# Transposing norms and probabilities by VectorE blocks and a DRAM detour instead of by TensorE, in a Perceiver block

## The chip, the cores and the metric

The kernel runs on one core of one Trainium2 chip. The metric is the device time of one execution in microseconds (us). A profile shows one execution: its span runs from the first to the last instruction, and the time of that execution is a little longer than the span. The engines are TensorE (PE, whose weight loads the profile lists apart as PEld), VectorE (DVE), ScalarE (ACT), GpSimd (POOL) and SyncE (SP, which here only issues DMAs).

## The reference

One layer over 16 batches, all in float32. Each batch has 128 tokens of 512 features and a context of 2048 rows of 512 features.

```
x = x + xattn(layernorm(x), ctx)     # softmax(h ctx^T) ctx: no scale, no projection
x = x + attn(layernorm(x), ...)      # 16 heads of 32; q, k, v by down and up weights;
                                     # rotary on half of each head; causal softmax; @ Wc
h = layernorm(x)
x = x + h + sum_e gate_e * (h A_e^T) Bw_e^T   # 8 experts of rank 64; the top 2 by the logits
                                              # of the batch's first token
```

In this setup the batch length S equals 128, so one batch of tokens fills the 128 partitions of one tile.

## The kernel before

The work is written as four Python generators per batch: `score` (first norm, context scores, softmax numerators), `attend` (product with the context, first residual, second norm), `inner` (self-attention, second residual, third norm) and `experts` (routing and the two chosen experts). A hand-written list of `step(kind, b)` calls at the end of `perceiver_block` interleaves the pieces of several batches. TensorE's instructions are kept in that written order (`tc.keep_in_program_order`), so TensorE runs them one after another in exactly that order, and a matmul whose input is late holds up all later ones. The DVE, ACT and POOL queues are ordered by the framework near the written order, and each engine works through its queue in order as well. In the steady part of the loop the loads on SP are not held to the written order (`written = False`).

For each batch TensorE does, by the names that the profile shows:

- `psc`: context scores, 4 tiles of 512 context rows, 16 matmuls each, from the transposed context `ctxT` (loaded) and the transposed norm `hT`;
- `tr_m` and `spread`: a shared maximum per token, turned and spread over the partitions; `den`: the softmax denominators;
- `av`: probabilities times context, 4 tiles `ctx`, 4 matmuls each;
- `q`, `k`, `v`: projections of the second norm with weights folded at the start (`fold_*`); `pss_sc`, `pss_acc`: the scores of 16 heads; `y`: probabilities times values per head; `o`: the output projection;
- `lg`: the 8 router logits; `mid`, `ffn`: the two experts;
- `tr` and `tr_p_a`: transposes by a matmul against the identity. Every float32 matmul is two passes in the profile, a transpose is one.

The transposes work in groups of four 128x128 blocks. `transposed(src, dst, name)` turns a norm of 128x512 into one PSUM bank and ScalarE copies the bank to SBUF (`hT1` for the first norm, `hT2` for the second, `hT3` for the third). `turn` does the same for four heads of the attention probabilities `att`, four times a batch. The attention softmax of a batch runs on DVE and ACT in four groups of four heads: mask add, maximum, 16 exponentials with sums on ACT, reciprocal, multiply.

The routing goes: `hT3` (its first column is the first token) -> `shares` on DVE (`g_share`, `g_part`) -> the matmul `lg` -> about a dozen small DVE instructions -> two indirect DMAs on POOL for the rows of `A` and one for `BT`. `early` does this routing for the last batch from the value row of the first token, ahead of the rest.

Buffers that matter: `ctx` and `ctxT` have four tiles of 1 MB each, so each tile can be loaded again as soon as the TensorE work on its predecessor is over; `ps_acc` has three PSUM banks and `ps_sc` two.

Of the kernel before, what the change touches and what calls it, by code (L numbers as in the profile page):

```python
# [29 lines left out]
SCALE = 1.0 / math.sqrt(DH)  # L30
NEG = -1e30


C_ID, C_MASK, C_COS, C_SIN, C_BLK = 0, 128, 256, 384, 512


C_ONE, C_TWO, C_ONER, C_TWOR, C_RANK, C_P = 514, 515, 516, 517, 518, 519
C_N = 520
# [4 lines left out]
def constants():  # L43

    c = np.zeros((P, C_N), np.float32)
    c[:, C_ID : C_ID + P] = np.eye(P)
# [20 lines left out]
def perceiver_block(ctx: ExitStack, tc: tile.TileContext, io: dict, out: bass.AP):  # L67
# [6 lines left out]
    p4 = ctx.enter_context(tc.tile_pool(name="p4", bufs=4))  # L74
    ps_tr = ctx.enter_context(tc.tile_pool(name="ps_tr", bufs=3, space=PSUM))
# [5 lines left out]
    ident = cst[:, C_ID : C_ID + P]  # L81
# [13 lines left out]
    written = True  # L95

    def load(*args):
        dma = nc.sync.dma_start(*args)
        if written:
            tc.keep_in_program_order(dma)  # L100
# [7 lines left out]
    def layernorm(src, name, n=P, tag="h"):  # L108
        stats = p2.tile([P, 6], F32, tag="stats", name=f"st_{name}")[:n]
        nc.vector.bn_stats(stats, src)  # L110
        mv = p2.tile([P, 2], F32, tag="mv", name=f"mv_{name}")[:n]
        nc.vector.bn_aggr(mv, stats)  # L112
        rstd = p2.tile([P, 1], F32, tag="rstd", name=f"rs_{name}")[:n]
        nc.gpsimd.tensor_scalar_add(rstd, mv[:, 1:2], EPS)  # L114
        nc.gpsimd.tensor_tensor(rstd, rstd, mhalf[:n], ALU.pow)  # L115
        h = (p2 if tag == "h" else p1).tile([P, D], F32, tag=tag, name=f"{tag}_{name}")[:n]
        nc.vector.tensor_scalar(h, src, mv[:, 0:1], rstd, ALU.subtract, ALU.mult)  # L117
        return h

    def transposed(src, dst, name, at=(0, 1, 2, 3)):  # L120

        tr = bank(ps_tr, "tr", f"tr_{name}")
        for c, i in enumerate(at):
            transpose(tr[:, c * P : (c + 1) * P], src[:, i * P : (i + 1) * P], ident)
        nc.scalar.copy(dst, tr.rearrange("p (c t) -> p c t", c=4))  # L125

    def turn(src, at, name):
        t = p4.tile([P, 4, P], F32, tag="pT", name=f"pT_{name}")
        transposed(src, t, f"p_{name}", at)
        return t  # L130
# [21 lines left out]
    def fold_products(i, n, g):  # L152
# [8 lines left out]
        folded = []  # L161
        for j, ps in enumerate(banks):
            t = p4.tile([P, D], F32, tag="pT", name=f"folded_{n}_{g}_{j}")
            (nc.vector.tensor_copy if j else nc.scalar.copy)(t, ps)
            folded.append(t)
        return folded
# [39 lines left out]
    def score(b):  # L206
# [3 lines left out]
        hT = p2.tile([P, KC, S], F32, tag="hT1", name=f"hT1_{b}")  # L210
        transposed(h, hT, f"1_{b}")
# [4 lines left out]
        for v, ct in enumerate(turned_cts.pop(b)):  # L216
            ps = bank(ps_sc, "sc", f"psc_{b}_{v}").rearrange("p (j t) -> p j t", j=4)
            for j in range(4):
                for c in range(KC):
                    matmul(  # L220
                        ps[:, j, :], ct[:, c, j * P : (j + 1) * P], hT[:, c, :],
# [62 lines left out]
    def inner(b):  # L284

        x1, h = firsts.pop(b)
        hT = p1.tile([P, KC, S], F32, tag="hT2", name=f"hT2_{b}")
        transposed(h, hT, f"2_{b}")
        yield

        heads_first = {}
        for n in ("q", "k"):
            ps = bank(ps_acc, "acc", f"{n}_{b}")
            for m in range(HC):
                for c in range(KC):
                    matmul(
                        ps[:, m * P : (m + 1) * P], w[n][:, c, m * P : (m + 1) * P], hT[:, c, :],
                        start=(c == 0), stop=(c == KC - 1),
                    )
            partner = p1.tile([P, HC, S], F32, tag=f"{n}P", name=f"{n}P_{b}")  # L300
            nc.vector.stream_shuffle(partner.rearrange("p c t -> p (c t)"), ps, PARTNERS)
            t = p1.tile([P, HC, S], F32, tag=f"{n}T", name=f"{n}T_{b}")
# [8 lines left out]
            heads_first[n] = t  # L311
            yield
        qT, kT = heads_first["q"], heads_first["k"]
        vv = p2.tile([P, D], F32, tag="vv", name=f"vv_{b}")
        att = p1.tile([P, H, S], F32, tag="att", name=f"att_{b}")
        nmx = p2.tile([P, H], F32, tag="nmx", name=f"nmx_{b}")
        sm = p2.tile([P, H], F32, tag="sm", name=f"sm_{b}")
        rsm = p2.tile([P, H], F32, tag="rsm", name=f"rsm_{b}")

        def project():  # L320

            ps = bank(ps_acc, "acc", f"v_{b}")
            for c in range(KC):
                matmul(ps, hT[:, c, :], w["v"][:, c, :], start=(c == 0), stop=(c == KC - 1))
            nc.scalar.copy(vv, ps)
            values[b] = (x1, vv)

        def compare():
# [25 lines left out]
            for group, ps in enumerate(pss):  # L354
# [17 lines left out]
                )  # L372


        for part in (project, compare) if b < B - 1 else (compare, project):
            part()
            yield

        flat = att.rearrange("p h t -> p (h t)")

        def heads(c):
            first = c // 2 * 8 + c % 2 * 2
            return first, first + 1, first + 4, first + 5

        now = [turn(flat, heads(c), f"a_{b}_{c}") for c in range(HC)]
        yield
        acc = bank(ps_acc, "acc", f"y_{b}")
        for c in range(HC):
            for j in range(4):
                at = c * P + j * DH  # L390
                matmul(
                    acc[j * DH : (j + 1) * DH, c * P : (c + 1) * P],
                    vv[:, at : at + DH], now[c][:, j, :], start=True, stop=True,
# [70 lines left out]
    def early(b):  # L464


        x1, vv = values[b]
# [8 lines left out]
        column = column_of(vv[:1, :], f"v0_{b}")  # L476
        v0 = small(b, KC, "v0")
        nc.vector.tensor_copy(v0, column)
# [13 lines left out]
    def experts(b):  # L492

        x2, h = lasts.pop(b)
        res = p2.tile([P, D], F32, tag="res", name=f"res_{b}")
        nc.gpsimd.tensor_tensor(res, x2, h, ALU.add)
        hT = p2.tile([P, KC, S], F32, tag="hT3", name=f"hT3_{b}")
        transposed(h, hT, f"3_{b}")
        yield
        if b not in routes:  # L500
            route(b, shares(b, hT[:, :, 0]))
# [3 lines left out]
        for c in range(KC):  # L505
            matmul(ps[:, :S], wa[:, c, :], hT[:, c, :], start=(c == 0), stop=(c == KC - 1))
# [3 lines left out]
        o = p2.tile([P, D], F32, tag="o", name=f"out_{b}")  # L510
# [24 lines left out]

    load_x(0)
    load_turned(0, [0])
    load_x(1)
    load_turned(0, [1, 2, 3])
    for v in range(VC):  # L540
        load_turned(1, [v])
        load_ctx(0, [v])
    load(up, io["up"])
    step(score, 0, 5)
    step(score, 1, 2)
    step(score, 0)
# [8 lines left out]
    step(score, 1)  # L555
    step(attend, 0)
    step(score, 1)
    load_weight("v", "ctx")
    step(attend, 0, 2)
    load_x(2)  # L560
    step(score, 2)
# [10 lines left out]
    for i, n, g in halves:  # L572
# [3 lines left out]
        ready = (n, g, folded)  # L576
    step(inner, 0)
    fold_turned(*ready)

    written = False  # L580
    for b in range(B - 2):
        if 2 < b + 2 < B:
            load_turned(b + 2)
        step(inner, b, 2)
        step(experts, b - 1)
        step(score, b + 2)
        step(inner, b)
        step(experts, b - 1)
        step(score, b + 1)
        step(score, b + 2, 2)  # L590
        step(attend, b + 1)
        step(inner, b)
        step(score, b + 2)
        step(attend, b + 1)
        step(score, b + 2)
        step(attend, b + 1)
        step(inner, b)
        step(score, b + 2)
        step(attend, b + 1)
        if b + 2 < B:  # L600
            load_ctx(b + 2)
        if b + 3 < B:
            load_x(b + 3)
        step(inner, b)
        step(experts, b - 1)
        step(inner, b)
        step(inner, b + 1)
        step(experts, b - 1)
        step(score, b + 3)
# [3 lines left out]
    step(inner, y)  # L613
    step(score, z)
    step(inner, y)
    step(experts, y - 1)
    step(inner, y)
    step(experts, y - 1)
    step(attend, z)
# [7 lines left out]
    step(inner, z, 2)  # L627
    step(inner, y)
    step(inner, z, 2)
    step(experts, y)  # L630
    step(early, z)
    step(experts, y)
    step(early, z)
    step(inner, z)
    step(early, z)
    step(inner, z)
# [46 lines left out]
```

## Time and profile before

| what | value |
|---|---|
| time, median of 3 runs (lowest, highest) | 880.22 us (880.09, 880.26) |
| time of the profiled execution | 879.31 us |
| its span | 875.8 us |
| PE busy | 846.8 us, 97% of the span |
| PEld, DVE busy | 615.6 us, 511.5 us |
| ACT, POOL busy | 270.9 us, 171.3 us |
| granted TensorE clock, mean over the span | 0.991 of full speed |
| DMA | 159.57 MB, mean 182 GB/s |
| HBM read, written | 154.47 MB, 4.19 MB |

The profile's page gives, part by part: busy time of each engine, the span in 40 slices, the DMA queues, the chain of work that ended last, groups of equal instructions with their mean duration and the wait ahead of them, and the DMA issues with the time to landing. The trace can also be asked for a timeline of one engine, for the sums of a window, and for the waits of one engine for another.

### The profile page before, as it was taken

Reading aid. Unit: us, or ns where it says so; the run is one execution under the profiler, and the core shown is the slowest. Engines: PE = TensorE matmul, PEld = TensorE weight load, DVE = VectorE, ACT = ScalarE, POOL = GpSimd, SP = SyncE. Lnnn points to the kernel's source line nnn. Section 1 sums busy time; section 2 is a strip of 40 time slices with the busy share of each in tenths; the row PEclk is TensorE's granted clock in tenths of the full one; section 3 lists DMA queues with packets and bytes.
Section 4 is the critical chain, followed back from the end, with each engine's and each line's share of the span. In section 5 each row is a group of like instructions: output and inputs, shape, how many; then the busy total and the mean of one; then the engine's idle time right before and its main releaser. Section 6 shows DMA issues by size and latency. Waiting matters only on the chain.

```text
span 875.8 us, 14131 instructions
## 1 busy us (share of the span) xinstructions
PE 846.8 (97%) x5498; PEld 615.6 (70%) x5498; DVE 511.5 (58%) x1234; ACT 270.9 (31%) x829; POOL 171.3 (20%) x232
## 2 busy tenths in 40 slices
PE   5999999999999999999999999999999999998966
PEld 4958767677777768677776867777686777765733
DVE  1436557375755747575574757557475755738472
ACT  1213314224232422423242242324224232422341
POOL 1001021130313103031310403121040312103123
PEclk9999999999999999999999999999999999999987
DMA  6997735637183563618356361835637183241001
GB/s 270 414 377 303 277 116 205 223 133 243 69 296 133 200 222 138 241 71 296 133 197 225 132 245 71 294 136 195 227 133 245 68 295 126 74 144 36 13 24 49
DMA packets 29553, 159.57 MB, mean 182 GB/s; under 512 B 4144, under 2 KB 4400, under 8 KB 13104
## 3 DMA queue, kind: packets, MB, share of 16 engines
q1 hardware_dynamic: 25392, 146.09, 45.7%
q0 software_dynamic: 4096, 12.59, 3.9%
q8 instruction: 43, 0.70, 0.3%
q14 instruction: 22, 0.18, 0.1%
HBM read 154.47 MB, written 4.19 MB: 181 GB/s over the span
## 4 chain that ended last, share of the span: by engine, by line
PE 93%; DVE 3%; POOL 1%; ACT 1%; issue 1%; DMA 1%; SPq 0%; ACTq 0%; POOLq 0%
PE psc L89 27%; PE av L89 25%; PE o L89 7%; PE q L89 6%; PE k L89 6%; PE v L89 5%; PE tr_p_a L92 3%; PE tr L92 2%; PE y L89 2%; PE pss_sc L89 2%; PE mid L89 2%; PE pss_acc L89 1%; PE ffn L89 1%; ACT att L365 1%; DMA x<-in_x_dram 1%
## 5 line engine op out<-in xcount | busy, mean ns | idle before, releaser
L89 PEld LDWEIGHTS psc<-hT,ctxT 128*128 128x128 f32 x2048 | 235.9, 193 | 12.9 <-DVE att L356 4.6
L89 PE MATMUL psc<-hT,ctxT 128*128 128x128 f32 x2048 | 240.2, 277 | 0.7 <-ACT hT L125 0.7
L89 PE MATMUL av<-ctx,sc 128*128 128x512 f32 x512 | 230.4, 593 | 0.0
L89 PEld LDWEIGHTS av<-ctx,sc 128*128 128x128 f32 x512 | 93.1, 192 | 92.9 <-issue 92.9
L365 ACT ACTIVATE att<-att,nmx 128x128 f32<-128x128 f32 x256 | 99.0, 389 | 113.8 <-DVE nmx L363 113.8
L114 POOL TENSOR_SCALAR rs<-mv 128x1 f32<-128x1 f32 x48 | 10.3, 226 | 435.4 <-DVE mv L112 435.0
L125 ACT COPY hT<-tr 128x512 f32<-128x512 f32 x48 | 26.8, 586 | 174.3 <-PE tr L92 174.3
L224 ACT COPY sc<-psc 128x512 f32<-128x512 f32 x64 | 37.1, 580 | 102.4 <-PE psc L89 101.9
L89 PEld LDWEIGHTS q<-hT,w_q 128*128 128x128 f32 x512 | 58.4, 192 | 10.2 <-ACT hT L125 10.2
L89 PE MATMUL q<-hT,w_q 128*128 128x128 f32 x512 | 61.3, 278 | 0.7 <-ACT hT L125 0.7
L89 PE MATMUL o<-w_c,yT 128*128 128x512 f32 x128 | 60.2, 615 | 0.9 <-ACT yT L396 0.9
L117 DVE TENSOR_SCALAR h<-x,mv,rs 128x512 f32<-128x512 f32 x48 | 39.3, 818 | 36.8 <-POOL rs L115 35.8
L89 PE MATMUL k<-hT,w_k 128*128 128x128 f32 x512 | 59.8, 275 | 0.0
L89 PEld LDWEIGHTS k<-hT,w_k 128*128 128x128 f32 x512 | 58.5, 192 | 0.0
L89 PE MATMUL v<-w_v,hT 128*128 128x512 f32 x128 | 57.7, 593 | 0.0
L441 POOL DMA_INDIRECT each<-in_A_dram,g_blocks x32 | 35.5, 1109 | 99.2 <-DVE g_dn L458 94.4
L125 ACT COPY pT_a<-tr_p_a 128x512 f32<-128x512 f32 x64 | 32.9, 600 | 53.0 <-PE tr_p_a L92 52.9
L365 ACT ACTIVATION_READ_ACCUMULATOR att<-att,nmx 128x1 f32 x256 | 48.2, 188 | 0.0
L356 DVE TENSOR_TENSOR att<-pss_sc,cst 128x512 f32<-128x512 f32 x32 | 20.6, 684 | 46.8 <-PE pss_sc L89 46.8
L249 DVE TENSOR_TENSOR sc<-sc,spread 128x512 f32<-128x512 f32 x64 | 42.6, 678 | 5.2 <-PE spread L89 5.2
L252 ACT ACTIVATE sc<-sc 128x512 f32<-128x512 f32 x64 | 40.2, 631 | 16.6 <-DVE sc L249 15.7
L370 DVE TENSOR_TENSOR att<-att,rsm 128x512 f32<-128x512 f32 x64 | 44.1, 689 | 1.1
(125 smaller groups left out, 952.3 us busy)
## 6 DMA issues: line engine op xcount, KB each, us to landing
ctxT<-in_ctxT_dram SPq DMA_DIRECT2D x64, 1024.0 KB, 4.8
ctx<-in_ctx_dram SPq DMA_DIRECT2D x64, 1024.0 KB, 4.8
x<-in_x_dram SPq DMA_DIRECT2D x16, 256.0 KB, 4.8
out_dram<-out POOLq DMA_DIRECT2D x15, 256.0 KB, 2.4
down_q<-in_Wq_downT_dram SPq DMA_DIRECT2D x2, 1024.0 KB, 11.4
down_k<-in_Wk_downT_dram SPq DMA_DIRECT2D x2, 1024.0 KB, 7.8
down_v<-in_Wv_downT_dram SPq DMA_DIRECT2D x2, 1024.0 KB, 7.9
w_c<-in_Wc_dram SPq DMA_DIRECT2D x1, 1024.0 KB, 13.3
```

What stands on the lines that cost most here:

```text
L89: tc.keep_in_program_order(nc.tensor.matmul(*args, **kwargs))
L92: tc.keep_in_program_order(nc.tensor.transpose(*args))
L114: nc.gpsimd.tensor_scalar_add(rstd, mv[:, 1:2], EPS)
L117: nc.vector.tensor_scalar(h, src, mv[:, 0:1], rstd, ALU.subtract, ALU.mult)
L125: nc.scalar.copy(dst, tr.rearrange("p (c t) -> p c t", c=4))
L224: nc.scalar.copy(sc[:, v], ps)
L249: nc.vector.tensor_tensor(sc[:, v], sc[:, v], spread[:, None, :S].to_broadcast([P, 4, S]), ALU.add)
L252: nc.scalar.activation(sc[:, v], sc[:, v], AF.Exp)
L356: nc.vector.tensor_tensor(att[:, hs, :], ps.rearrange("p (h t) -> p h t", h=4), cst[:, None, C_MASK : C_MASK + S].to_broadcast([P, 4, S]), ...
L365: nc.scalar.activation(att[:, i, :], att[:, i, :], AF.Exp, bias=nmx[:, i : i + 1], scale=SCALE, accum_out=sm[:, i : i + 1],)
L370: nc.vector.tensor_tensor(att[:, hs, :], att[:, hs, :], rsm[:, hs, None].to_broadcast([P, 4, S]), ALU.mult)
L441: nc.gpsimd.indirect_dma_start(each[:, i, :], None, io["A"], bass.IndirectOffsetOnAxis(ap=blocks[:, i : i + 1], axis=0),)
```

## The change

Four things change together.

**Who transposes.** For most batches `transposed` no longer uses TensorE and ScalarE. VectorE transposes the 32x32 blocks inside each group of 32 partitions (`nc.vector.transpose`, one instruction for 128x512), into a tile `blocks` (for norms) or `pX` (for probabilities, two groups of four heads each). `send` then writes the four groups of partitions to a DRAM tile `there` with four DMAs, and `fetch` reads it back with one DMA, so that each block reaches the partitions where it belongs. All five go onto SP's queue. This is done for `hT1` of batches 1 to 15, `hT2` of batches 0 to 14, `hT3` of batches 0 to 13, and the probabilities of batches 0 to 13 (two halves a batch). The remaining transposes, at the start and in the last two batches, stay on TensorE.

**Layouts.** The turned tiles are now laid out by group of 32 tokens (`hT[p, a, c, j]`). The matmuls that stream them read them with a stride. `v`, which loads them as weights, is split into four column groups: 16 matmuls of 32 weight columns in place of 4 of 128.

**The order.** The step list is new: `v` ahead of `k` and `q`; all four `psc` tiles of a batch in a row; `y` of batch b after the `psc` tiles of batch b+2; the router's `lg` of batch b-1 between the second `av` tile of batch b+1 and the head scores of batch b; and the loads, sends and fetches on SP all held to the written order. For the first two norms POOL's steps are held to the order in which they are written.

**Small edits.** The identity is a tile of its own, loaded by ScalarE's queue; `early` computes the first token's values with 16 matmuls of one column from `hT2`; several tiles have one buffer where they had two.

```diff
+    def send(name):
+        if name not in ways:
+            return
+        blocks, dst = ways[name]
+        n = blocks.shape[2]
+        there = dram.tile([4, QD, 4, n * QD], F32, tag=f"there_{n}", name=f"there_{name}")
+        for a in range(4):
+            load(
+                there[:, :, a, :].rearrange("q i e -> i q e"),
+                blocks[a * QD : (a + 1) * QD].rearrange("i q n j -> i q (n j)"),
+            )
+        ways[name] = there, dst
+
+    def fetch(name):
+        if name in ways:
+            there, dst = ways.pop(name)
+            load(dst.rearrange("p a n j -> p (a n j)"), there.rearrange("q i a e -> (q i) (a e)"))
...
+        else:
+            blocks = p1.tile([P, 4, n, QD], F32, tag="blocks", name=f"blocks_{name}")
+            nc.vector.transpose(blocks, src.rearrange("p (n q i) -> p q n i", n=n, q=4))
+            ways[name] = blocks, dst
...
+            ps = bank(ps_acc, "acc", f"v_{b}")
+            for c in range(KC):
+                for a in range(4):
+                    matmul(
+                        ps[a * QD : (a + 1) * QD, :], hT[:, a, c, :], w["v"][:, c, :],
+                        start=(c == 0), stop=(c == KC - 1),
+                    )
...
+                if group % 2 == 0:
+                    blocks = p2.tile([P, 4, H // 2, QD], F32, tag="pX", name=f"pX_{b}_{group}")
+                nc.vector.transpose(
+                    blocks[:, :, group % 2 * 4 : group % 2 * 4 + 4, :],
+                    att[:, hs, :].rearrange("p n (q i) -> p q n i", q=4),
+                )
+                if group % 2:
+                    ways[f"p_{b}_{group // 2}"] = blocks, pT[group // 2]
...
     for b in range(B - 2):
...
         step(inner, b, 2)
         step(experts, b - 1)
+        send(f"3_{b - 1}")
+        if b:
+            load_turned(b + 2, [0])
+        fetch(f"3_{b - 1}")
+        if b:
+            load_turned(b + 2, [1, 2, 3])
+        step(attend, b + 1, 2)
+        load_ctx(b + 2, [0, 1])
+        step(experts, b - 1)
+        step(inner, b)
+        step(attend, b + 1)
+        load_ctx(b + 2, [2])
+        step(attend, b + 1)
+        step(inner, b + 1)
+        send(f"p_{b}_0")
+        load_ctx(b + 2, [3])
+        fetch(f"p_{b}_0")
+        send(f"2_{b + 1}")
+        send(f"p_{b}_1")
+        fetch(f"2_{b + 1}")
+        fetch(f"p_{b}_1")
+        if b + 3 < B:
+            load_x(b + 3)
+        step(score, b + 2, 4)
+        step(inner, b)
+        step(inner, b + 1)
         step(score, b + 2)
         step(experts, b - 1)
+        step(score, b + 3, 2)
+        send(f"1_{b + 3}")
+        fetch(f"1_{b + 3}")
         step(inner, b)
         step(score, b + 2)
         step(experts, b - 1)
```

The steps of `inner` in the changed kernel are, in this order: turning the second norm, `v`, `k`, `q`, the head scores with their softmax, (in the last two batches turning the probabilities,) `y`, `o`. Those of `experts` are: turning the third norm, routing, `mid`, `ffn`.

## The prediction

> **What bounds the kernel now.** I read the busy times and the chain of waits first, then one steady batch as a window, then that batch on the PE timeline, then the tail's waits beside the granted clock, last the DMA issues. A change of 0.2% (1.8 us) is about what a measurement of this kernel can tell from none.
>
> ```profile
> PE 846.8 (97%) x5498; PEld 615.6 (70%) x5498; DVE 511.5 (58%) x1234; ACT 270.9 (31%) x829; POOL 171.3 (20%) x232
> PE 93%; DVE 3%; POOL 1%; ACT 1%; issue 1%; DMA 1%; SPq 0%; ACTq 0%; POOLq 0%
> ```
>
> ```profile
> 338.20:389.35 51.15, 51.15 (x336) 37.60 (x335) 31.61 (x76) 16.46 (x52) 10.62 (x14) 1.00 0.52 186
> ```
>
> The window is one batch, from one `psc` start to the next: PE is busy all 51.15 us, DVE 31.6, DMA 52%. So the steady part is bound by PE, and a batch costs what PE does in it. PE work that goes is gained whole; a PE wait that appears is lost whole, because TensorE keeps the written order.
>
> **What is removed.** The PE timeline of that batch:
>
> ```profile
> 364.92 1.97 PE L92 MATMUL tr_p_a<-cst,att 128*128 128x128 f32 x16
> 366.72 0.32 PE L92 MATMUL tr_m<-cst,mx 128*128 128x128 f32 x1
> ...
> 370.41 1.08 PE L89 MATMUL y<-pT_a,vv 128*32 128x128 f32 x32
> ...
> 375.85 0.60 PE L92 MATMUL tr<-cst,h 128*128 128x128 f32 x4
> 376.29 1.02 PE L89 MATMUL ffn<-wb,mid 128*128 128x512 f32 x2
> 377.18 3.84 PE L89 MATMUL q<-hT,w_q 128*128 128x128 f32 x32
> 380.86 3.74 PE L89 MATMUL k<-hT,w_k 128*128 128x128 f32 x32
> ```
>
> From start to next start, the 16 transposes of probabilities take 1.80 us and four of a norm 0.44. A batch loses 1.80 + 3 x 0.44 = 3.1 us of PE, so 51.15 becomes 48.05. The seven ACT copies that go (0.59 each) cost nothing, ACT being idle 68% of the batch.
>
> **What costs nothing, or little.** `v` becomes 32 passes of 32 weight columns by 512. If the four column groups overlap, it stays at 3.44 us; if not, 4 x 3.44. `y` has that shape of weights: 32 passes in 1.08 us, 0.27 of it the last one's latency, so 25 ns each, where `q` needs 3.68 / 32 = 115 ns for as many columns. They overlap, so 3.44; the other end, +10.3 us a batch, is a rival. The extra DMA is 7 transfers of 256 or 512 KB a batch each way, 3.5 MB on 9.5 (186 GB/s x 51.15): 13.0 MB in 48 us is 271 GB/s, and this trace moved 427 for 10 us, so bandwidth holds. The seven DVE transposes appear nowhere in the trace. The nearest row, the shuffle of 128x512, has 0.72 us, net 0.62 between starts; half or twice that moves DVE by 2 to 5 us of some 36 in 48. I take 0.62, and count them only on the two paths below.
>
> **The wait added at `lg`.** The listing of the built program shows the queues. On DVE, after `o` of batch b: residual, third norm, the softmax adds and sums of batch b+2, `k` rotation, `q` shuffle and multiply, and only then the transpose of the third norm. On SP: four sends, the load of `ctxT` tile 0, the fetch of `hT3`. Then DVE `g_share`, `g_part`, and PE `lg`; behind `lg` wait the head scores, the rest of `av` and all later PE work. Before, `hT3` came from PE directly and `v` covered its routing.
>
> PE gets from the end of `o` to `lg` in spread 0.3 + ffn 0.9 + k and q 7.3 + two `av` 6.9 = 15.4 us. The other way:
> - DVE: 17 full-width operations at 0.61 net (two mask adds start 349.90 and end 1.29 later), 0.8 for small ones, 0.2 to start: 11.4.
> - Sends: an SP issue takes 0.33 to 0.43; the fourth starts 1.2 later and lands 1.8 after that (the small output store): 14.4.
> - Fetch: 256 KB alone lands in 2.7. Here 1 MB went ahead at 12.9 and lands 4.8 later, at 17.7; the rest is behind it, 0.65 at 400 GB/s: 18.4. Alone, 17.1.
> - `g_share` 0.93 and `g_part` 0.18: 19.5.
>
> So `lg` comes 4.1 us late; with a freer queue and faster DVE 2.5, with DVE at its recorded 0.69 each 5.5.
>
> ```profile
> x<-in_x_dram SPq DMA_DIRECT2D x16, 256.0 KB, 4.8
> ...
> out_dram<-out SPq DMA_DIRECT2D x2, 128.0 KB, 1.8
> ```
>
> ```profile
> ctxT<-in_ctxT_dram SPq DMA_DIRECT2D x64, 1024.0 KB, 4.8
> ```
>
> The median 4.8 of `x` is that of a load queued behind 1 MB; its minimum is 2.7.
>
> The shuffle's row, 0.72 us for 128x512, is what I use for a DVE transpose. The Trainium skill (VectorE: DVE Perf Modes, "The three transpose paths" and "Rules for kernel authors") says that VectorE transposes only 32x32 blocks and sends whole 128x128 transposes to TensorE, which speaks against this change; from its 311 ns for 128x128 in bf16 I estimate 1.24 us for 128x512, by which `lg` would come 0.6 us later still.
>
> **The wait added at `y`.** After `lg`, DVE does the routing (2.3 us) before the softmax of the heads, so the first mask add starts 2.35 after `lg`. Counted from that add: the old timeline has the first exponential 2.9 later (352.83) and 1.55 of ACT for a group of four heads, so the groups' sums are there at 4.5, 6.05, 7.6 and 9.15. On DVE group 0 is then multiplied by 6.0 and transposed by 6.9, group 1 by 7.5 and 8.3, group 2 by 9.0 and 9.7; the first residual goes to 10.5, group 3's multiply to 11.1, the norm's statistics to 11.7, group 3's transpose to 12.4; aggregate, POOL (1.26 from aggregate to norm), norm and its transpose end at 15.1. SP sends the second norm ahead of the second half of the probabilities: eight issues from 15.2, the last lands at 19.8, the fetch of 512 KB takes 3.3 (2.7 plus 256 KB): 23.1, so 25.4 after `lg`. PE comes to the second half of `y` after lg 0.14 + scores 1.93 + two `av` with `den` 7.0 + four `psc` 14.3 + half of `y` 0.5 = 23.9. Wait 1.6 us; 0 if DMAs land 1.5 sooner, 3 if issues take 0.43 and landings 2.4. `hT2` for `v` is there 2 us earlier.
>
> **The clock.** The same trace shows what PE waits do besides:
>
> ```profile
> 800.03 0.36 PE L89 MATMUL lg<-g_part,ones 128*128 128x8 f32 x2 [2.32 <-DVE g_part L419]
> ...
> 842.03 1.25 PE L89 MATMUL tr_v<-ones,vv 1*128 1x1 f32 x8 [3.61 <-ACT vv L325]
> ```
>
> ```profile
> 800.00:806.00 6.00, 5.97 (x27) 3.34 (x28) 3.50 (x18) 0.29 (x1) 3.02 (x3) 1.00 0.15 44
> ...
> 842.00:844.00 2.00, 1.25 (x8) 1.17 (x8) 1.01 (x4) 2.00 (x11) 0.00 (x0) 0.68 0.00 0
> 844.00:847.00 3.00, 0.60 (x3) 0.57 (x4) 1.65 (x5) 1.54 (x7) 0.00 (x0) 0.50 0.00 0
> 847.00:852.00 5.00, 5.00 (x10) 0.90 (x11) 1.99 (x14) 0.29 (x1) 2.97 (x3) 0.74 0.17 52
> ```
>
> After a gap of 2.32 us the clock (third number from the right) stays at 1.00; after 3.61 it is at 0.5 from about 842.7 (0.68 as mean of 842 to 844) to 849.6 (0.74 as mean of 847 to 852), some 6.9 us, in which PE loses 3.4 us of work. A wait of 4.1 lies over that, one of 2.5 under. The Trainium skill (TensorE: Matmul & The Clock Gate, "Why this matters for your kernels") says to leave no PE gap over about 3 us, which speaks against this change; its windows run freely, so that a gap little over a window halves the clock only at times. I take half of the batches. Where the clock halves, the 3.4 us lie ahead of `y` and cover its 1.6, a net 1.8; on average 0.9.
>
> **The sum.** A batch: 48.05 + 4.1 + 1.6 + 0.9 = 54.65, or 3.5 more than now. There are 13 such batches between the `psc` starts of batches 2 and 15: +45.5. Start: POOL now finishes the first norm before the second (h at 9.35 could start at about 5.4), but `hT1` of batch 1 has one buffer and waits for all `psc` of batch 0, and its `ctxT` is queued behind that fetch; together -3. Tail: -2.7 of transposes, +5.2 because `lg` of batch 13 has only one `av` ahead (7.5 in place of 2.3), +1.6 at `y`, -5 for `early`, which no longer needs `vv`: -1. So 875.8 - 3 + 45.5 - 1 = 917.3 of span; 3.5 lie outside the span (879.31), and the median is 0.9 above this execution: 921.7, say 921.
>
> **Rivals.**
> - *Both round trips are hidden.* For it: 15 and 24 us of PE work cover them, and my paths overrun by only 4.1 and 1.6 in long sums. Against: every step is a measured row and in one queue. Then a batch is 48.05: 13 x -3.1 = -40, start -3, tail -2.7: 834.5 + 3.5, about 838. The sign turns where the two waits and the clock together are 3.1 us a batch. Faster at all: 0.19.
> - *The clock halves in every batch.* 48.05 + 4.1 + 3.4 = 55.55, and with `lg` 5.5 late 57: 13 x 4.4 to 5.9, and 3 in the tail: 934 to 956. 0.19.
> - *Column groups of `v` do not overlap.* 10.3 x 16 = 165 more, though it would delay nothing else: about 1080. The row of `y` speaks against it. 0.02.
> - *Forecast*, with `lg` 2.9 to 5 late and `y` 0.5 to 2: 890 to 934. 0.58. Within 0.2% by chance: 0.02.
>
> **How the numbers follow.** Range: low end 48.05 + 2.5 + 0 = 50.55, 13 x -0.6, start and tail -4: 868. High end: the clock rival's 956. Below 868 lie full hiding and most of what comes near it, about 0.13; above 956, 0.05. Slower: 0.58 + 0.19 + 0.02 = 0.79; faster 0.19.
>
> **What would show it.** Right: `tr_p_a` gone from the chain; a steady batch of 53 to 56 us; `lg` waiting 3 to 5 us for `g_part`, and DVE `g_share` waiting for the DMA into `hT3`; `y` waiting for a DMA into `pT` by 0 to 3 us; `v` still 3.4 to 3.6 us; granted clock below 0.99 where `lg` waits over 3.5 us. Wrong: a steady batch near 48 with PE busy throughout; or the `g_share` wait gone because the DVE work ahead is shorter than 11.4 us; or a wait I did not count, such as `psc` tile 3 waiting for DVE's maximum (margin 1.7 us), or the loads of `ctx` coming late behind SP's waits.

## The result, and the profile after

The changed kernel took 1015.6 us (median of 4 runs, 1009.8 to 1019.0) against 880.15 us for the kernel before on the same chip: ratio 1.154, 95% interval 1.148 to 1.159. The forecast of 921 us had the sign right and the size far too small; the range ended at 956.

The busy times, and the chain of waits by engine and by its heaviest lines, from the page of the changed kernel:

```profile
PE 859.4 (85%) x5506; PEld 599.1 (59%) x5506; DVE 575.9 (57%) x1334; ACT 222.4 (22%) x729; POOL 168.4 (17%) x232
PE 43%; DMA 30%; DVE 12%; SPq 7%; ACT 6%; issue 3%; POOL 0%; DVEq 0%; ACTq 0%
```

PE's share fell from 97% to 85%, and its part of the chain from 93% to 43%: DMAs, DVE and SP's queue have taken its place. The waits (engine and group, what it waited for, us in total, times, longest) name two places:

```profile
PE lg L91 <- DVE g_part L469: 101.2, 15, 8.2
DVE g_share L463 <- DMA hT<-there: 80.1, 14, 6.6
PE y L91 <- DMA pT<-there_p: 28.5, 14, 3.3
PE v L91 <- DMA hT<-there: 2.2, 1, 2.2
```

So `lg` waits 7.2 us on average in 14 batches and `y` 2.0; in the steady part the first and second norms' detours cost nothing. One steady batch as a window, then its PE timeline. A window row gives the stretch and its length, then the busy time of PE, PEld, DVE, ACT and POOL, the granted clock, the busy share of the DMA engines (1 is all of them) and their GB/s; a timeline row gives start and duration, and in brackets the wait ahead and what ended it.

```profile
304.96:364.00 59.04, 50.65 (x333) 35.81 (x329) 36.06 (x85) 13.04 (x44) 10.41 (x14) 0.94 0.61 223
```

```profile
321.04 7.03 PE L91 MATMUL av<-ctx,sc 128*128 128x512 f32 x16
334.72 0.59 PE L91 MATMUL lg<-g_part,ones 128*128 128x8 f32 x2 [6.64 <-DVE g_part L469]
335.24 2.08 PE L91 MATMUL pss_sc<-kb,qT 64*128 64x256 f32 x8
...
346.58 14.46 PE L91 MATMUL psc<-hT,ctxT 128*128 128x128 f32 x128
360.96 0.64 PE L91 MATMUL y<-pT,vv 128*32 128x128 f32 x16
363.35 0.64 PE L91 MATMUL y<-pT,vv 128*32 128x128 f32 x16 [1.75 <-DMA pT<-there_p]
363.81 3.62 PE L91 MATMUL v<-w_v,hT 128*32 128x512 f32 x32
```

The batch is 59.04 us where it was 51.15: 50.65 of PE, 6.64 ahead of `lg` and 1.75 ahead of `y`. PE's 50.65 is 2.6 more than the 48.05 of work left to it, because the clock is halved behind `lg` (0.59 from 332 to 338). `v` at full clock takes 3.62 with its last one's latency, as forecast. The first wait, from the end of `o` (312.98) on DVE and SP:

```profile
313.02 0.69 DVE L452 TENSOR_TENSOR x<-o,x 128x512 f32<-128x512 f32 x1 [3.72 <-PE o L91]
325.88 0.70 DVE L159 STREAM_TRANSPOSE blocks<-h 128x512 f32<-128x512 f32 x1
329.82 0.34 SPq L98 DMA_DIRECT2D hT<-there  x1
334.23 0.21 DVE L463 TENSOR_TENSOR g_share<-w_r,hT 128x32 f32<-128x32 f32 x1 [5.36 <-DMA hT<-there]
```

Where the 139.7 us of span went: 138.6 lie between the first `fold_q` matmul and `lg` of batch 13 (742.3 us before, 880.9 after), 4.8 ahead of them, and the tail behind gives 3.7 back.

**One ruler for all runs.** The work of a batch forms a ring: each piece waits for the one before, and the next batch's first piece for this one's last. The ring is cut here into three arcs, and two detours lie in it: from the end of `o` (its result gives the third norm) to the start of `lg`; from there (behind `lg` stands the heads' softmax on DVE) to the end of `y`; from there to the end of the next `o`. Means over 10 to 12 steady batches of each trace, in us; their sum is the batch:

| kernel | `o` to `lg` | `lg` to `y` | `y` to `o` | batch | time |
|---|---|---|---|---|---|
| forecast (without its 0.9 for the clock) | 19.5 | 26.0 | 8.0 | 53.5 | 921 |
| changed | 22.2 | 29.7 | 8.9 | 60.9 | 1015.6 |
| third norm by TensorE | 15.4 | 27.5 | 8.7 | 51.6 | 882.4 |
| probabilities by TensorE | 22.2 | 29.0 | 8.0 | 59.2 | 995.4 |
| third norm earlier | 16.4 | 29.9 | 9.4 | 55.7 | 949.7 |
| no residual on GpSimd | 20.5 | 29.6 | 8.5 | 58.6 | 985.2 |
| idle work at `lg` | 22.3 | 29.5 | 9.6 | 61.4 | 1022.3 |
| `v` first only | 22.5 | 30.9 | 4.6 | 58.0 | 975.9 |
| `ctx` late, `x` first | 22.2 | 28.0 | 8.0 | 58.2 | 982.2 |
| norms 1 and 2 by the detour only | 15.4 | 26.6 | 8.0 | 50.0 | 867.1 |
| third norm by TensorE, `v` first | 15.4 | 28.8 | 4.6 | 48.8 | 850.7 |

(Where `v` stands ahead of `y`, its 3.4 us belong to the second arc.) Where PE waits for nothing the first arc is 15.4 and the third 8.0; the second is then 26.6 with 1.8 of `tr_p` in it, so 24.8 without.

### The profile page after: what moved, and what is told of

It is laid out like the page before. It is cut to its first block, busy times and chain, and to the rows that moved or that the text cites. A ratio compares the mean times of both kernels' runs of the same rounds, so it can differ in the third digit from the quotient of the medians.

```text
span 1015.5 us, 14652 instructions
## 1 busy us (share of the span) xinstructions
PE 859.4 (85%) x5506; PEld 599.1 (59%) x5506; DVE 575.9 (57%) x1334; ACT 222.4 (22%) x729; POOL 168.4 (17%) x232
## 4 chain that ended last, share of the span: by engine, by line
PE 43%; DMA 30%; DVE 12%; SPq 7%; ACT 6%; issue 3%; POOL 0%; DVEq 0%; ACTq 0%
DMA there_p<-pX 12%; DMA pT<-there_p 8%; PE av L91 7%; DMA hT<-there 7%; PE v L91 7%; SPq L98 7%; PE o L91 5%; PE k L91 5%; PE q L91 5%; ACT att L400 5%; PE psc L91 3%; PE pss_sc L91 3%; DMA there<-blocks 3%; DVE att L391 2%; DVE nmx L397 2%
## 5 line engine op out<-in xcount | busy, mean ns | idle before, releaser
L91 PE MATMUL psc<-hT,ctxT 128*128 128x128 f32 x2048 | 236.1, 278 | 7.1 <-DMA ctxT<-in_ctxT_dram 6.4
L91 PE MATMUL av<-ctx,sc 128*128 128x512 f32 x512 | 236.2, 610 | 0.5 <-DMA ctx<-in_ctx_dram 0.5
L91 PEld LDWEIGHTS av<-ctx,sc 128*128 128x128 f32 x512 | 96.6, 197 | 111.7 <-issue 110.6
L91 PE MATMUL lg<-g_part,ones 128*128 128x8 f32 x32 | 9.3, 364 | 101.2 <-DVE g_part L469 101.2
L112 POOL TENSOR_SCALAR rs<-mv 128x1 f32<-128x1 f32 x48 | 10.8, 224 | 507.0 <-DVE mv L110 507.0
L91 PEld LDWEIGHTS lg<-g_part,ones 128*128 128x128 f32 x32 | 7.8, 303 | 113.2 <-DVE g_part L469 112.0
L257 DVE TENSOR_TENSOR mx<-psc,mx 128x512 f32<-128x512 f32 x32 | 22.1, 691 | 91.2 <-ACT sc L254 91.2
L91 PE MATMUL v<-w_v,hT 128*32 128x512 f32 x512 | 71.7, 710 | 2.2 <-DMA hT<-there 2.2
L507 ACT ACTIVATE g_ex<-g_top,g_nm 128x1 f32<-128x1 f32 x16 | 4.7, 294 | 254.1 <-DVE g_nm L506 254.1
L285 DVE TENSOR_TENSOR sums<-sc,sums 128x512 f32<-128x512 f32 x32 | 51.2, 1599 | 0.2
L117 DVE TENSOR_SCALAR h<-x,mv,rs 128x512 f32<-128x512 f32 x48 | 26.2, 546 | 39.4 <-POOL rs L115 39.4
```

What stands on the lines that cost most here:

```text
L91: tc.keep_in_program_order(nc.tensor.matmul(*args, **kwargs))
L112: eps = nc.gpsimd.tensor_scalar_add(rstd, mv[:, 1:2], EPS)
L257: nc.vector.tensor_tensor(mx, ps, mx if v > 1 else sc[:, 0], ALU.max)
L285: nc.vector.tensor_tensor(sums, sc[:, v], sums if v > 1 else sc[:, 0], ALU.add)
```

## The experiments

**Which detour costs.** Four runs give transposes back to TensorE, in the changed kernel's order and layouts.

```diff
# norm3_by_tensor: this line alone; all_by_tensor: the like for all norms and the probabilities
# (where the probabilities are turned by TensorE, that stands ahead of the last psc tile)
-        transposed(h, hT, f"3_{b}", b >= B - 2)
+        transposed(h, hT, f"3_{b}", True)
# all_by_tensor_2: also
-        step(inner, b + 1)          # behind the last av
+        step(inner, b + 1, 2)       # behind y of batch b
```

> The changed order of a batch's work, the layouts by group of 32 tokens and the split `v` stay; every norm and all probabilities are transposed by TensorE again, so nothing goes through DRAM. Theory: the loss is made by the two detours alone, so a steady batch is again what PE does, about 51.2 us, `v` 3.4 to 3.6 us, granted clock 0.99, and the time 875 to 890 us. Rival: the new order or the layouts cost by themselves (operands read with a stride, `v` in column groups, DVE's new order); then a good part of the 135 us stays: over 920 us.

981.9 us, ratio 1.117 (1.115 to 1.118): the theory missed, and the time is in the rival's range. The trace shows one place of the new order, not the layouts:

```profile
PE tr L94 <- DVE h L117: 93.4, 20, 6.2
```

With TensorE, the second norm's transpose stood right behind the `av` whose result the norm needs. The place was made for the detour; TensorE waits 5.4 us there in each steady batch (the 6.2 is the longest wait, at the start). So this run told of its own edit, and was made again with that one transpose behind `y`:

> All transposes by TensorE as in the run before, but the transposes of the second norm stand behind `y` in TensorE's order instead of right behind the last `av`, where they waited 6.2 us for the norm's h in each batch. Theory: that wait, and the clock halved after it, were the whole price of the new order, and the layouts cost nothing: a steady batch of about 51.2 us, granted clock 0.99, 875 to 890 us. Rival: the strided operands or the column groups of `v` cost PE time even so; PE's busy time at full clock stays over 865 us and the time over 900 us.

899.9 us (ratio 1.021 to 1.024), batch 52.0. The first two arcs are at PE's floor and the clock is 1.00; the 0.85 over 51.15 is `v` waiting for the ScalarE copy of the transpose right ahead of it (0.7 to 1.0 a batch). Transposes at the start also wait 17 us for their norms, where the kernel before waits 10.8. Strided operands and the column groups of `v` cost nothing: four `psc` tiles take 14.45 us, `v` 3.64. The theory's 890 was missed by 10, its claim on the layouts holds: PE is busy 51.24 us in a batch of this run, and 51.15 before.

> Only the third norm is transposed by TensorE; the other norms and the probabilities keep the detour. Theory: the wait at `lg` (about 7 us a batch) goes, and with it the clock loss after it (some 3 us a batch); PE gets 0.44 back; the wait at `y` stays and no longer finds a late PE, so it may grow from 2 to 3 or 4 us and halve the clock in some batches: 13 x (7 + 3 - 0.44 - 2) = about 100 us off, 900 to 935 us. Rival: SP's queue and the DMA backlog set the pace, so that PE waits the same time elsewhere: over 970 us.

882.4 us, ratio 1.002 (0.999 to 1.004), better than the theory or its rival: of the 135 us lost, 133 come back by 14 x 4 transposes. The wait at `lg` is gone, the first arc is 15.4; `y` still waits 2.3 us a batch. The second arc fell by 2.2 as well: the fetch of the first half of the probabilities goes out 4.4 us behind the first of its sends, in place of 7.5 (means of 11 batches). In the changed kernel SP stands behind the third norm, and the loads of `ctxT` and `ctx` stand behind SP, so this one detour also makes the other late; the section on the prediction has the rows.

> Only the probabilities are transposed by TensorE; the three norms keep the detour. Theory: the wait at `y` (2 us a batch) and the second halving of the clock go, PE does 1.8 us more, and `lg` still waits about 7 us a batch with the clock halved behind it: 990 to 1010 us. Rival: the eight sends of the probabilities with 3.5 MB of DMA traffic are what makes the fetch of the third norm late; then the wait at `lg` falls by 2 us or more and the time to 960 us or less.

995.4 us (1.130 to 1.134): as the theory said. The first arc keeps its 22.2, so the probabilities' sends do not delay the third norm's fetch.

> Third norm and probabilities by TensorE, first and second norm by VectorE and the detour. Theory: nothing is left in the ring, so a batch is PE's work alone: 51.15 - 2 x 0.44 = 50.3 us; 13 x -0.9 = -11, start -3 and tail about 0: 863 to 868 us. Rival: the first or second norm's detour is late too; 875 us or more.

867.1 us, ratio 0.987 (0.986 to 0.989), batch 50.0, PE busy throughout, as forecast: the part of the change that is well covered is worth 1.3%.

**The first arc.** 

```diff
# norm3_earlier
+        step(experts, b - 1)
+        send(f"3_{b - 1}") ... fetch(f"3_{b - 1}") ...
         step(inner, b, 2)
-        step(experts, b - 1)
-        send(f"3_{b - 1}") ... fetch(f"3_{b - 1}") ...
# no_residual_on_gpsimd
-        res = p1.tile([P, D], F32, tag="res", name=f"res_{b}")
-        nc.gpsimd.tensor_tensor(res, x2, h, ALU.add)
+        res = x2
```

> Only the order changes: the experts' first step of batch b-1 with its send and fetch is written ahead of the k and q steps of batch b, so that DVE transposes the third norm some 3 operations (and the wait for them) earlier; TensorE's order is the same, and all transposes stay with VectorE and the detour. Theory: `lg` is late because its transpose stands late in DVE's queue, behind the sums and the k and q rotation; 4 to 5 us earlier leaves a wait of 2 to 3 us at which the clock is not halved: 13 x (4.5 + 3) = about 97 us off, 905 to 940 us. Rival: the fetch behind the backlog of loads is the binding step and lands no earlier; over 980 us.

949.7 us (1.075 to 1.085), 10 us above the theory's range. The first arc fell by 5.8 to 16.4, more than expected; but the second did not move (29.9 for 29.7), so what PE no longer lost at `lg` it lost at `y`:

```profile
PE y L91 <- DMA pT<-there_p: 58.9, 14, 6.3
PE lg L91 <- DVE g_part L469: 25.0, 15, 8.3
```

The arcs give the time by themselves: 5.2 a batch x 13 = 68, measured 66.

> The changed kernel without the add `res` on GpSimd; the last residual takes x2 alone, so the norm's term h is left out of the output. Theory: DVE's second `sums` takes 2.9 us instead of 0.7 because GpSimd runs two adds beside it; with one left (`kP`) it takes about 1.6, the third norm's transpose comes 1.1 to 1.3 us earlier, `lg` waits 5.7 us instead of 7.0, 13 x 1.2 = 16 us off: 995 to 1003 us. If `sums` falls to 0.7, 2.2 x 13 = 29 us: about 987. Rival: `sums` is slow by itself (its operands), and the time stays within 5 us of 1015.

985.2 us (1.117 to 1.122): the second of the theory's two cases. In the changed kernel, DVE's timeline and beside it GpSimd's:

```profile
318.85 0.68 DVE L285 TENSOR_TENSOR sums<-sc,sums 128x512 f32<-128x512 f32 x1
320.08 2.91 DVE L285 TENSOR_TENSOR sums<-sc,sums 128x512 f32<-128x512 f32 x1
```

```profile
319.93 1.28 POOL L552 TENSOR_TENSOR res<-x,h 128x512 f32<-128x512 f32 x1
321.16 1.27 POOL L358 TENSOR_TENSOR kP<-kP,cst 128x512 f32<-128x512 f32 x1
```

The same add takes 0.68 alone and 2.91 when it starts 0.15 behind GpSimd's: it ends 0.56 behind the end of the second GpSimd one (322.43). Without `res`, from DVE and GpSimd of that run:

```profile
316.53 0.67 DVE L285 TENSOR_TENSOR sums<-sc,sums 128x512 f32<-128x512 f32 x1
```

```profile
316.72 1.61 POOL L358 TENSOR_TENSOR kP<-kP,cst 128x512 f32<-128x512 f32 x1 [0.38 <-DVE kP L353]
```

Now DVE is first, and GpSimd's multiply is the longer one. The Trainium skill (SBUF — State Buffer, "Who interferes with whom") states this: a VectorE instruction with two SBUF inputs and a GpSimd instruction that reads SBUF want the same ports, and the one that starts first keeps them while the other stands still. The rows agree. The forecast took 0.61 for this operation, and it was 2.2 to 2.3 longer; taking the cause away made the first arc 1.7 shorter and the batch 2.3.

**The clock.** Seven useless matmuls fill most of the gap ahead of `lg`:

```diff
+            if b < B - 2:
+                idle = bank(ps_tr, "tr", f"idle_{b}")
+                for _ in range(7):
+                    matmul(idle, w["c"][:, 0, :P], w["c"][:, 1, :], start=True, stop=True)
             route(b, shares(b, hT[:, 0, :, 0]))
```

> The changed kernel with seven useless float32 matmuls of 512 columns (about 6.0 us at full clock) just ahead of `lg` in batches 0 to 13, where TensorE otherwise stands still for some 7 us. Theory: the halved clock behind `lg` is the gap's doing; with the gap cut to about 1 us the clock stays at 1.00, the 2.5 to 3 us of PE work lost there come back in the batches where `y` does not take them up again, and the kernel gets faster although TensorE does 84 us more work: 13 x 1 to 3, 975 to 1005 us. Rival: the clock is halved for another reason, or what is gained is all waited for again at `y`: 1010 us or more.

1022.3 us (1.159 to 1.165): the rival's end. The clock did what the theory said (third number from the right, the stretch behind `lg`: changed kernel, then this run):

```profile
332.00:338.00 6.00, 3.28 (x16) 2.74 (x18) 2.89 (x17) 0.29 (x1) 1.05 (x1) 0.59 1.00 411
```

```profile
333.00:339.00 6.00, 4.75 (x25) 2.71 (x24) 2.35 (x15) 0.29 (x1) 0.66 (x1) 1.00 0.96 382
```

But both arcs stayed (22.3 and 29.5): `y` waited 57.3 us in place of 28.5. The second arc is set by the softmax and its detour, not by PE, so PE's clock in it costs nothing here, and neither do the 6 us of extra PE work in the first arc.

**The second arc.**

```diff
# v_first_only (vv gets two buffers)
         step(score, b + 2, 4)
+        step(inner, b + 1)
         step(inner, b)
-        step(inner, b + 1)
# ctx_loads_late; ctx_late_x_first has load_x(b + 3) ahead of it
-        load_ctx(b + 2, [0, 1]) ... load_ctx(b + 2, [2]) ... load_ctx(b + 2, [3])
         fetch(f"p_{b}_1")
+        load_ctx(b + 2)
```

> The changed kernel with all its detours, and only `v` of the next batch written ahead of `y` (two buffers for `vv`). Theory: the two detours lie in one ring, from `o` by the third norm to `lg` (21.7 us in the trace), from `lg` by the softmax and the probabilities' detour to the second half of `y` (28.6), and from there by the rest of `y`, `v`, `tr_m`, `mid` to the end of `o` (8.7): 59.0 us, the batch. Taking `v` out of the ring makes it 3.5 us shorter: 13 x 3.5 = 46 off 1016, about 970 us. Rival: the waits of TensorE simply add up with its work; then only the wait at `y` (2.0 us a batch) is covered and `lg` stays: 988 us or more.

975.9 us (1.109 to 1.113), 6 above the theory and 12 below the rival. `y` waits for nothing now; the second arc, with `v` in it, is PE's own work at a clock halved behind `lg`. At full clock that work is 24.8 + 3.4 = 28.2, and the arc is 30.9: where no detour sets the arc, the halved clock costs 2.7.

> The changed kernel with the four `ctx` loads of batch b+2 moved on SP's queue behind the second fetch of the probabilities; nothing else. Theory: the first half's sends land 5.5 us after issue because 4 MB of loads are queued ahead of them, and SP stands still behind them; with the loads later they land in about 2.5 us, the second half's fetch lands some 2.5 us earlier, and the ring is shorter by that: 13 x 2.5 = 33 off 1016, about 983 us. Rival: sends are slow by themselves (many short rows), or the later loads collide with the norms' fetches or reach `av` late: 1008 us or more.

1020.4 us (1.157 to 1.162): missed, by a fault of the edit. The sends did land in 2.3 us, but `x` was now queued behind 4 MB, the first norm fell between `o` and the third norm on DVE, and the first arc grew to 25.3; `av` also stood 13.7 us in all, for what the trace doesn't say. With `x` ahead:

> The changed kernel with the four `ctx` loads of batch b+2 behind the second fetch of the probabilities and behind the load of `x` (in the run before, `x` stood behind the 4 MB and landed after 13 us, so that the first norm fell into DVE's stretch between `o` and `lg` and made `lg` 2.8 us later). Theory: the arc from `lg` to `y` is shorter by the 2 to 2.5 us that the sends and the fetch gain, with `lg` as late as in the changed kernel: 1016 - 13 x 2.2 = about 987 us. Rival: the backlog was no cause, or the loads now come late for `av`: 1008 us or more.

982.2 us (1.114 to 1.119), as expected. The DMA issues (KB each, median us to landing), changed kernel and this run:

```profile
there_p<-pX SPq DMA_DIRECT2D x112, 128.0 KB, 5.4
```

```profile
there_p<-pX SPq DMA_DIRECT2D x112, 128.0 KB, 2.3
```

These medians are over both halves. By halves, the sends of the first land 6.0 us after issue in the changed kernel and those of the second 2.7; in this run both take 2.3. A stretch of the changed kernel in which the first half's sends are under way (345.35 to 352.26) shows what they stand behind:

```profile
345.00:352.00 7.00, 7.00 (x54) 6.04 (x53) 5.62 (x12) 1.92 (x9) 1.07 (x3) 1.00 1.03 407
```

All DMA engines are busy, at 407 GB/s. In this run the same stage (339.68 to 343.39) has a share of 0.55 and 141 GB/s. The first arc is as before, the second 1.7 shorter, and the third 0.9, because `v` no longer runs at a halved clock behind a wait of `y` (in the changed kernel it takes up to 6.1 us in place of 3.6): 2.6 x 13 = 34, measured 33.

**Mended versions.** `norm3_tensor_v_first` is `norm3_by_tensor` with `v` ahead of `y`; the next has `mid` ahead of both.

> The third norm by TensorE as in the run before, and `v` of the next batch (with two buffers for `vv`) written ahead of `y`. Theory: in that run the second half of `y` waited 2.3 to 3.6 us a batch for its fetch, and the clock was halved behind the longer waits; the norm's fetch lands ahead of the probabilities' second one, so `v` (3.5 us) covers the wait. A batch is then near 48.5 us: 13 x -2.7 = 35 below the kernel before, less start and tail gains of a few us: 838 to 855 us. Rival: `v` now waits for its own fetch instead, as late as `y` was: 870 us or more.

850.7 us, ratio 0.966 (0.964 to 0.969): the fastest kernel of the study, 165 us below the changed one. One batch:

```profile
316.13:365.47 49.34, 48.26 (x333) 34.95 (x333) 35.97 (x83) 13.79 (x46) 10.38 (x14) 1.00 0.75 255
```

PE is busy 48.26 of 49.34 us at full clock.

> Third norm by TensorE, probabilities and the other norms by the detour, and TensorE's order behind the last `psc` is `mid`, `v`, `y`. Theory: in the run with `v` first it still waited 0.6 to 1.1 us a batch for the second norm's fetch; `mid` (0.9 us) covers most of it: 13 x 0.8 = 10 off 850.7, about 841 us. Rival: `v` waits as long behind `mid`, because the ring by the fetch moves with it: 849 us or more.

854.7 us (0.970 to 0.974): no gain. `v` waits 3.6 us in all where it waited 10.6, but `o` now waits 7.4 for ScalarE's copy of `y`, which `mid` had covered.

The last three keep every transpose of the change on VectorE and move places only. The first two add `v` first, and `v` first with late `ctx`, to `norm3_earlier`.

> All transposes of the change stay with VectorE and the detour; only order is changed, in two places: the third norm's transpose ahead of the k and q steps, and `v` ahead of `y`. Theory: `lg` waits 1 to 2.5 us (as in the run with the third norm earlier), too little to halve the clock each time, and `y` is covered by `v` but for 1 to 2 us: a batch of 48.1 + 1.7 + 1.5 = 51.3 us, 875 to 895 us. Rival: what is gained in one arc is lost in the other again, as with the third norm earlier alone: over 915 us.

899.8 us (1.022 to 1.026), a little over the theory: arcs 16.4, 30.8, 4.6.

> As the run before, and the `ctx` loads behind the probabilities' second fetch and the `x` load. Theory: the fetches land 2 us earlier, so that `v` and `y` wait for nothing; only `lg` waits 1 to 2.5 us: 48.1 + 1.7 = 49.8 us a batch, 855 to 875 us, faster than the kernel before with every transpose of the change still on VectorE. Rival: the later `ctx` loads collide with the third norm's sends and fetch, and `lg` waits 4 us or more: 890 us or more.

932.7 us (1.059 to 1.063): the rival's time, and `lg` waits some 4 us as it said, but for another reason than DMAs that collide. In this build the framework put the third norm's transpose behind the slow `sums` on DVE again; the first arc is 19.3.

```diff
# norm3_at_once_v_first: v first, res added in place into x2, and
         step(inner, b)              # y's copy and o
+        step(experts, b)
+        send(f"3_{b}") ... fetch(f"3_{b}") ...
         step(score, b + 2)
```

> All transposes of the change stay with VectorE and the detour. The experts' first step of batch b, with its send and fetch, stands directly behind the step of `o`, so that DVE transposes the third norm right behind the norm, ahead of the sums; the residual `res` is added in place into `x2` (room for it), and `v` stands ahead of `y`. Theory: the places in the queues decide, not the detour: the transpose ends some 5.5 us behind `o`, the fetch lands at about 12 to 13, and TensorE comes to `lg` only at 15.4; `lg` does not wait, `v` waits about 1 us, the clock stays at 1.00: 49 us a batch, 845 to 858 us. Rival: the detours with all their DMAs are late anyway, `lg` or `v` waits 2 us or more: 870 us or more.

873.6 us, ratio 0.992 (0.989 to 0.994). The first arc is at its floor, 15.2, as the theory said; a batch is 50.6, because the second arc is 30.7 by `v`'s wait (1.9 us a batch) and a clock that some of the short gaps still halve. The time is 16 us above the theory's range and in the rival's (870 or more), whose reason, a wait of 2 us at `v`, is nearly what was found. The loads of `ctxT` moved with the sends, so the run doesn't tell the places apart. What it shows is that the whole change, with other places in the queues, takes 0.8% less than the kernel before in place of 15% more.

## Why the prediction was wrong, step by step

Three terms failed: one DVE add at 0.61 that took 2.9, the eight issues and their landing at 19.8, and the order of loads and sends on SP, which was put at nothing. The steps in turn:

- *PE-bound, 48.05 us of work left*: right. One batch of the last run has 48.05 us of PE in 49.42.
- *`v` at 3.44, DVE transposes at 0.62*: right (0.70 us for 128x512 with its latency). The estimate from the Trainium skill (VectorE: DVE Perf Modes, "The three transpose paths"), 1.24, was twice too high.
- *"Bandwidth holds"*: right as a mean (223 GB/s in the batch shown), wrong where it counts. From 332 to 352, until the first half of the probabilities has landed, the DMA engines are fully busy (shares 1.00, 1.01 and 1.03). The term put at nothing was the order on SP: SP waits for the third norm's blocks with the loads behind them, the DMA engines are idle from 322 to 326, and 7 loads of 1 MB are then issued ahead of the probabilities' sends. With the third norm by TensorE the DMA engines are fully busy already 14 to 6 us ahead of `lg`. The forecast named loads "behind SP's waits" only as a sign of being wrong. The changed kernel's row of SP's waits:

```profile
SPq L98 <- DVE blocks L159: 335.1, 29, 27.2
```

- *`lg` 4.1 us late (2.5 to 5.5)*: the mechanism was right, the size failed: 7.2. Of the 17 DVE operations one took 2.9, not 0.61. With that, 14.4 for the landing of the sends becomes 16.8, the fetch took 4.4 for 4.0, and `g_share` 0.21 in place of 0.93. The 0.93 itself was a sign overlooked: that row of the trace of before was a two-input multiply standing beside `kP` on GpSimd.
- *`y` 1.6 us late* (25.4 less 23.9 is 1.5): as a wait nearly right (2.0), by luck; as a step wrong. The arc was 29.7, not 26.0, and the wait stayed small only because PE came late too, at a halved clock. DVE was timed well: it had the turned norm 17.2 us behind `lg` (mean of 11 batches), where the forecast has 17.45. The failed term is the one behind it, "eight issues from 15.2, the last lands at 19.8; the fetch takes 3.3". The batch shown, where the first mask add starts at 337.35:

```profile
351.02 0.71 DVE L159 STREAM_TRANSPOSE blocks<-h 128x512 f32<-128x512 f32 x1
345.35 1.75 SPq L98 DMA_DIRECT2D there_p<-pX  x4
352.26 0.34 SPq L98 DMA_DIRECT2D pT<-there_p  x1
352.69 1.91 SPq L98 DMA_DIRECT2D there<-blocks  x4
354.64 2.86 SPq L98 DMA_DIRECT2D there_p<-pX  x4
359.41 0.34 SPq L98 DMA_DIRECT2D pT<-there_p  x1
```

SP stands until 352.26 for the landing of the first half, so the eight issues start behind it and not behind DVE. In means counted from `lg`, forecast and measured: the eight issues start at 17.55 and 18.55, the last of them at 20.35 and 22.4, the fetch goes at 22.15 and 25.2, the second half of `y` starts at 25.4 and 28.9. So 1.0 is the late start, 1.0 the slower issuing, 1.0 the landing and 0.4 the fetch. `ctx_late_x_first` shows that 1.7 of the arc comes back when the loads of `ctx` stand behind; there PE at its halved clock is near the arc, so more may be the backlog's. The issues stand some 0.48 apart, not 0.4, and in some batches the eighth stands up to 1.1 more; why was not tested.

- *The clock, 0.9 net*: wrong in kind. Behind `lg` it halves in every batch shown, but costs nothing there; it costs 0.9 at `v`, behind `y`. The rival "the clock halves in every batch" therefore named a thing that happened and a price that wasn't paid.
- *The sum*: 53.5 against 60.9. The arcs are 2.7, 3.7 and 0.9 longer; less the 0.9 set aside for the clock that is 6.4 x 13 = 83. The start lost 4.8 in place of gaining 3: a `ctxT` tile came 6.4 us late, issued behind the fetch of `hT1`, which the forecast had named and priced too low. The fourteenth `lg`, which the forecast had in its tail with 5.2, stands in the 138.6 us measured up to it: these are 138.6 - 45.5 - 5.2 = 88 over the forecast, the 83 and 5 more for the fourteenth pass. Behind it the tail gained 3.7, where the forecast without the 5.2 has 6.2. Together 7.8 + 88 + 2.5 = 98, and the span was 1015.5 - 917.3 = 98 over the forecast.
- In the rival "both round trips are hidden" the sum comes to 834, not 838: 3.5 was added twice. Nothing hangs on it.

The range failed because each bound stretched one wait at a time, with rows taken from stretches in which nothing stood beside the operation.

## What to carry to other kernels

When two late arrivals lie in one ring of dependences, add up the ring arc by arc, each arc as the longer of TensorE's work and the other engines' path: a clock loss or spare work inside an arc that another engine sets costs nothing, and shortening one arc leaves the other where it was, unless it also clears a queue that the other uses. Before moving work to VectorE and DMAs, list what stands ahead of it in each queue at that moment, GpSimd's operations beside it and loads already queued included; a row's duration holds only for the company it was measured in. Of several like edits, one may carry all the loss: here one norm's detour cost 133 of 135 us, and placing a transpose right behind its producer, or a consumer one step too early, was worth 82 us (`all_by_tensor`) and 32 us (`norm3_by_tensor`).

## What the runs showed of the hardware

- A two-input DVE add of 128x512 takes 0.68 us alone and 2.91 when it starts behind the first of two GpSimd operations that read SBUF; in the other order GpSimd's takes 1.61 for 1.27.
- A send of 128 KB to DRAM lands in 2.3 us, and in 6.0 while queued loads of 1 MB keep the DMA engines fully busy (407 GB/s).
- A DMA that waits for its data at the head of SP's queue holds up the loads behind it: SP stood 335 us for DVE's blocks, and the DMA engines were idle (0.00 from 322 to 326) with loads still to come.
- Shorter gaps than I had thought halve the clock. After waits of 2.44 us (`norm3_earlier`, 319.03) and 1.70 (`norm3_at_once_v_first`, 396.46), the window rows are:

```profile
322.00:326.00 4.00, 4.00 (x12) 1.90 (x9) 4.00 (x12) 1.85 (x9) 2.00 (x3) 0.56 1.01 425
```

```profile
398.00:402.00 4.00, 4.00 (x12) 1.91 (x9) 4.00 (x13) 1.30 (x7) 2.94 (x3) 0.57 1.01 426
```

In the steady parts of the 18 traces the shortest wait of TensorE with a halving beside it or within 3.6 us behind it is 1.66 us (`norm3_earlier`, 597.06); waits up to about 1.6 always left the clock at 1.00, and between 1.7 and 3.3 it went either way: 2.88 (`norm3_at_once_v_first`, 222.08) and 3.32 (`no_residual_on_gpsimd`, 359.50) did nothing, and neither did 2.32 in the kernel before. The Trainium skill (TensorE: Matmul & The Clock Gate, "Why this matters for your kernels") warns of gaps over about 3 us; in these runs 1.7 was enough at times, so the bound to plan with is lower.
